# Position terms as row and column sums, another order of first loads and of the last comparisons, in a two-layer attention kernel

## The chip, the cores and the metric

The kernel runs on one core of one Trainium2 chip. A core has five engines with a queue of instructions each: TensorE (PE, matrix products; its weight loads are shown as PEld), VectorE (DVE), ScalarE (ACT), GpSimd (POOL) and SyncE (SP, which only issues transfers). Sixteen DMA engines move data between the device memory and the core's own memory, SBUF; matrix products land in another one, PSUM. The metric is the device time of one execution in microseconds (us).

## The reference

The input x is (8, 128, 48, 48): 8 batches, 128 channels, N = 48 x 48 = 2304 places. Cut to what matters:

```python
# layer 0: group norm, 32 position channels, q, k, v, causal attention
x0 = concat([gn(x), pe]).reshape(B, 160, N)
q = lrelu(Wq @ x0 + bq); k = lrelu(Wk @ x0 + bk); v = lrelu(Wv @ x0 + bv)
attn = softmax(where(tril, q.T @ k / sqrt(128), -10000)) * tril
x = x + attn @ v
# layer 1: on tokens
t = t + softmax(ln(t) @ ln(t).T) @ ln(t)
wx = batch_norm(ln(t) @ W.T)                 # over all 8 * 2304 tokens
y[s] = sigmoid(wx[s] + y[s - 1] @ V.T)       # a recurrence over the 2304 places
x = t + y
```

The position channels pe are 16 channels that depend on the row of a place alone and 16 that depend on its column alone; they are the same in all batches.

## The kernel before

All work is in float32. A batch's 2304 places are cut into NQ = 6 chunks of QC = 384 (eight rows of the image each). One program of three stages runs: an opening, the attention stream over the eight batches, and the recurrence. A general path (for inputs beyond certain bounds) stands behind a flag that the end of the fast path computes.

*Opening.* The first batch's x is loaded in three pieces on SP's queue (L706, L708), weights and position rows on ACT's and SP's queues (L733 to L739). Twelve products of a unit matrix with itself, written by `idle`, run on PE meanwhile. `positions(n, j)` (L820) makes the position term plus bias of chunk n for q, k and v (j = 0, 1, 2): the product of the 33 position weights (wpT) with the 33 position rows (L830; for v, places and channels are exchanged, in three products, L833), then a copy by ACT (L834). The three parts of a chunk are stored to the device memory together (posb_d, L836), and `load_positions` (L838) loads them back for every use but the first two. Chunks 0 and 1 are made in tiles of their own; the later ones share the two buffers of the pool tpool, one of which holds wpT. `group_norm` (L782) computes mean and reciprocal root for the norm: statistics on DVE, two tiny products on PE, a power on POOL (L660).

*The stream.* `project(b, n)` (L848) makes q, k and v of one chunk: norm on DVE (L865), product (L872, L875), addition of the position term (L877), leaky relu (L882). At its end DVE takes the largest absolute value of q and k (L886, for the flag). Three chunks are projected ahead (EARLY = 3). The class Causal runs layer 0's attention over pairs of a chunk and a block of 128 keys: score product (L1011), exp on ACT (L1013), a mask on POOL where the block lies on the diagonal (L1016), output product (L1022) three items later (LAG = 3), row sums on DVE (L1033, L1037). The class Full runs layer 1's attention, the residual, the norm and the product with W.

The order is written out by the class Stream, which has a clock of its own: `now`, and the time at which each engine is free. Side work is a chain of steps, each with an estimated cost and a due time; after every item `tick` runs at most two steps, the first in the list that are due. `finish` runs a chain to its end at once and moves `now` to its due time; `advance` runs it up to a step. The order so made is the order of the instructions on every engine; at run time each engine takes them in that order and waits where it must. Score products, projections and idle products take their PSUM tiles in turn from four buffers (psum_s).

*The recurrence.* 96 segments of LS = 24 places run side by side in three groups (G = 3), each begun 12 places early. DVE writes the inputs of two places into PSUM (L1488 to L1495), PE adds the product with V (L1539), ACT takes the sigmoid (L1541). Before it, PE runs fourteen idle products (L1471). The result of two places plus the residual is written by `add_residual` (L1517): on POOL up to place LM = 20 of a segment, on DVE behind it (groups 1 and 2 read a residual tile t2s with a stride, group 0 a tile t2l); group 0's earlier places are added by a DMA that POOL issues (L1553). `seams` (L1509) compares each segment's last state with the state that its right neighbour reached in its early places; the flag follows from the largest difference (L1558 to L1565), and each engine branches on it (L1578, L1579).

Of the kernel before, what the change touches and what calls it, by code (L numbers as in the profile page):

```python
# [14 lines left out]
F32 = mybir.dt.float32  # L15
# [6 lines left out]
EMB = 16  # L22
# [10 lines left out]
def position_rows(side):  # L33

    pe = np.array(
        [
            [p / np.power(10000.0, 2 * (j // 2) / EMB) for j in range(EMB)] if p != 0 else np.zeros(EMB)
            for p in range(side)
        ]
    )  # L40
    pe[1:, 0::2] = np.sin(pe[1:, 0::2])
    pe[1:, 1::2] = np.cos(pe[1:, 1::2])
    t = pe.astype(np.float32).reshape(EMB, side)
    px = np.broadcast_to(t[:, :, None], (EMB, side, side))
    py = np.broadcast_to(t[:, None, :], (EMB, side, side))
    ones = np.ones((1, side, side), np.float32)
    return np.ascontiguousarray(np.concatenate([px, py, ones], axis=0).reshape(NPE + 1, side * side))

# [499 lines left out]
class Stream:  # L548
# [48 lines left out]

    def finish(self, chain):
        while chain.steps:
            self.run(chain)  # L600
        self.now = max(self.now, chain.at)
# [3 lines left out]
def fast_path(ctx: ExitStack, tc: tile.TileContext, x, pe, w_ffn, out, x_tok, w_qkv, w_pos, v_t, gamma_beta, flag):  # L605
# [56 lines left out]
    with ExitStack() as actx:  # L662
# [78 lines left out]
        def ffn_weights():  # L741
# [4 lines left out]
            nc.vector.tensor_scalar(w1, w1, s, None, ALU.subtract)  # L746
            tp = psum_t("tp_ffn")
            nc.tensor.transpose(tp[:, 0:P], w1, ident)
            nc.vector.tensor_copy(w1T, tp[:, 0:P])
# [68 lines left out]
        pos, pos_loads, made = {}, {}, {}  # L818

        def positions(n, j):  # L820

            if j == 0:
# [4 lines left out]
            pe_c = pe_sb[n // (NQ // 2)][: NPE + 1, ts(n % (NQ // 2), QC)]  # L827
            ps = psum_s(f"pb_{n}_{j}")
# [5 lines left out]
            nc.scalar.copy(made[n][:, j, :], ps[:, :QC])  # L834
            if j == 2:
                nc.sync.dma_start(posb_d[:, n], made[n])  # L836
# [11 lines left out]
        def project(b, n):  # L848
# [18 lines left out]
            def part(j):  # L867
                def f():
# [15 lines left out]
                    if j == 2:  # L884
                        for i in range(2):
                            nc.vector.tensor_reduce(  # L886
                                largest[b][:, i, n : n + 1], c[i], AX.X, ALU.max, apply_absolute_value=True
                            )
# [7 lines left out]

            steps = [(normed, 0.0, [("DVE", 0.75)])]

            steps += [(part(j), QC * US, [("DVE", 0.0 if j < 2 else 4.5)]) for j in range(3)]
# [82 lines left out]
        class Causal:  # L982
# [133 lines left out]
        class Full:  # L1116
# [115 lines left out]
            def after(self, j, o):  # L1232
# [4 lines left out]
                far = FULL_FAR and not last  # L1237
# [150 lines left out]
        st.add([(ffn_weights, 0.3, [("DVE", 0.5)])], 30.0)  # L1388
# [53 lines left out]
    with ExitStack() as rctx:  # L1442
# [3 lines left out]
        rlast = rctx.enter_context(tc.tile_pool(name="rlast", bufs=3))  # L1446
# [24 lines left out]
        idle(pw[:, 2 * P :], 14)  # L1471
# [44 lines left out]

        def add_residual(g, l0, yt):  # L1517
# [12 lines left out]
        for t in range(-WARM, LS):  # L1530
            s = t % TZ
            for g in range(G):
# [89 lines left out]
```

## Time and profile before

| | us |
|---|---|
| median of 6 runs | 1783.17 |
| lowest and highest run | 1779.44 and 1785.31 |
| the profiled execution's own time | 1784.57 |
| its span, first to last instruction | 1782.7 |
| PE busy in the span | 1746.1 |
| DVE busy | 1312.9 |
| ACT busy | 734.2 |
| POOL busy | 204.6 |
| mean granted clock of PE | 0.99 |
| first score product starts | 19.36 |
| last statistics of the stream done | 1707.4 |
| first product of the recurrence starts | 1713.30 |
| last sigmoid ends | 1760.68 |
| last DVE add ends | 1775.32 |

The profile is of one execution. A line of its timeline has the start, the time taken, the engine, the line of the kernel, the operation, what it writes and reads, how often, and in brackets how long the engine had been idle before and what ended that. A line of a stage has its bounds and length, then busy time and number of instructions for PE, PEld, DVE, ACT and POOL, then the granted clock of PE (1.00 is full speed), the busy share of the DMA engines and GB/s. A float32 product shows as two instructions.

### The profile page before, as it was taken

To read this page: it belongs to the slowest core of one execution; us is meant where nothing else is said; L and a number is where in the kernel's file an instruction comes from. 1 tells how busy PE (TensorE), PEld (TensorE's weight loads), DVE (VectorE), ACT (ScalarE), POOL (GpSimd) and SP (SyncE) were. 2 spreads that over 40 slices of the span, in tenths; PEclk is the share of its full clock that TensorE was granted. 3 is DMA by queue.
4 is the path that set the end of the run, shared out by engine and by line. 5 is a ranking of instruction groups with operands and counts; after the bars stand their busy time and mean duration, and the time that the engine had idled before them with its cause. 6 is when DMAs were issued, how large, how long until landed. Compare 5 with 4: busy or idle time off the path is not lost.

```text
span 1782.7 us, 22180 instructions
## 1 busy us (share of the span) xinstructions
PE 1746.1 (98%) x6243; PEld 1095.3 (61%) x6243; DVE 1312.9 (74%) x3361; ACT 734.2 (41%) x1812; POOL 204.6 (11%) x305
## 2 busy tenths in 40 slices
PE   8999999999999999999999999999999999999995
PEld 5666566665666566665666656665666656665574
DVE  4868668766887668786688668786687866876477
ACT  2344424443345423444244433454234442454354
POOL 1110011100110001100111001100011001100026
PEclk8999999999999999999999999999999999999998
DMA  3405672257423584056622574245830576125847
GB/s 138 139 23 177 183 198 93 84 183 192 128 93 133 164 222 125 23 190 182 194 86 88 183 188 127 93 133 164 221 124 23 191 186 178 47 89 182 206 174 199
DMA packets 205576, 256.10 MB, mean 144 GB/s; under 512 B 89889, under 2 KB 175042, under 8 KB 205444
## 3 DMA queue, kind: packets, MB, share of 16 engines
q1 hardware_dynamic: 204492, 251.57, 48.0%
q0 software_dynamic: 720, 2.62, 1.0%
q8 instruction: 52, 0.85, 0.2%
q14 instruction: 80, 0.66, 0.1%
q10 hardware_dynamic: 232, 0.40, 0.1%
HBM read 150.24 MB, written 104.27 MB: 143 GB/s over the span
## 4 chain that ended last, share of the span: by engine, by line
PE 96%; DVE 1%; DMA 1%; issue 0%; ACT 0%; POOL 0%; SPq 0%; ACTq 0%; DVEq 0%; POOLq 0%
PE s L1212 18%; PE o L1226 18%; PE s L1011 17%; PE o L1022 17%; PE o L1222 13%; PE pj L872 4%; PE pj L875 2%; PE wx L1319 2%; PE z L1539 2%; PE tb L932 1%; PE of_t L932 1%; PE pb L830 0%; DVE r L1521 0%; DMA x<-in_x_dram 0%; PE dn L1070 0%
## 5 line engine op out<-in xcount | busy, mean ns | idle before, releaser
L1214 ACT ACTIVATE p<-s,shift 128x384 f32<-128x384 f32 x504 | 292.3, 580 | 487.5 <-PE s L1212 472.2
L1013 ACT ACTIVATE p<-s 128x384 f32<-128x384 f32 (+2 forms) x504 | 231.7, 460 | 440.9 <-PE s L1011 389.0
L1212 PE MATMUL s<-xh 128*128 128x384 f32 x1008 | 410.4, 489 | 0.0
L1226 PE MATMUL o<-p,xhT 128*128 128x384 f32 x1008 | 404.0, 487 | 4.4 <-ACT p L1214 4.4
L1011 PE MATMUL s<-q,k 128*128 128x384 f32 (+2 forms) x1008 | 382.1, 461 | 0.7 <-DVE k L882 0.7
L1022 PE MATMUL o<-p,vT 128*128 128x384 f32 (+2 forms) x1008 | 378.0, 457 | 0.0
L1222 PE MATMUL o<-g,xhT 128*128 128x384 f32 x720 | 281.4, 488 | 0.8 <-DMA g<-e 0.7
L1226 PEld LDWEIGHTS o<-p,xhT 128*128 128x128 f32 x1008 | 189.0, 190 | 132.3 <-ACT p L1214 8.7
L1022 PEld LDWEIGHTS o<-p,vT 128*128 128x128 f32 x1008 | 189.1, 191 | 115.1 <-issue 1.2
L1212 PEld LDWEIGHTS s<-xh 128*128 128x128 f32 x1008 | 186.1, 190 | 115.0
L1011 PEld LDWEIGHTS s<-q,k 128*128 128x128 f32 x1008 | 182.9, 191 | 98.1 <-issue 1.7
L1037 DVE TENSOR_TENSOR acc<-acc,p 128x384 f32<-128x384 f32 (+2 forms) x408 | 209.0, 512 | 33.4 <-POOL p L1016 8.8
L1175 DVE STREAM_TRANSPOSE t<-p 128x384 f32<-128x384 f32 x360 | 187.3, 550 | 37.6 <-ACT p L1214 36.0
L1222 PEld LDWEIGHTS o<-g,xhT 128*128 128x128 f32 x720 | 133.1, 190 | 83.3 <-issue 1.8
L1183 DVE TENSOR_REDUCE tsum<-t 128x12 f32<-128x1152 f32 x120 | 162.4, 1353 | 4.2
L877 DVE TENSOR_TENSOR z<-pj,pb 128x384 f32<-128x384 f32 x144 | 78.9, 548 | 111.2 <-PE pj L872 92.9
L1016 POOL TENSOR_TENSOR p<-p,triu 128x128 f32<-128x128 f32 x144 | 72.3, 504 | 609.1 <-ACT p L1013 496.7
L1292 POOL TENSOR_TENSOR roots<-ve_f,mhalf 128x3 f32<-128x3 f32 x48 | 41.1, 856 | 521.4 <-DVE ve_f L916 521.4
L1214 ACT ACTIVATION_READ_ACCUMULATOR p<-s,shift 128x1 f32 x504 | 97.2, 193 | 0.0
L872 PE MATMUL pj<-xn,wT 128*128 128x384 f32 x192 | 80.4, 504 | 1.4 <-DVE xn L865 1.4
L922 POOL TENSOR_TENSOR rs_c<-ve_c,mhalf 128x3 f32<-128x3 f32 x48 | 45.1, 940 | 216.2 <-DVE ve_c L916 213.6
L1320 DVE TENSOR_TENSOR scale<-wx,scale 128x384 f32<-128x384 f32 x46 | 25.4, 552 | 56.5 <-PE wx L1319 55.8
(264 smaller groups left out, 1475.3 us busy)
## 6 DMA issues: line engine op xcount, KB each, us to landing
e<-t SPq DMA_DIRECT2D x120, 576.0 KB
g<-e SPq DMA_DIRECT2D x480, 144.0 KB
pb<-posb_d SPq DMA_DIRECT2D x46, 576.0 KB
t1t<-in_x_tok_dram SPq DMA_DIRECT2D x48, 192.0 KB
t_d<-tt SPq DMA_DIRECT2D x184, 48.0 KB
t2x<-t_d SPq DMA_DIRECT2D x46, 192.0 KB
scale<-rs SPq DMA_DIRECT2D x46, 192.0 KB
x<-in_x_dram SPq DMA_DIRECT2D x14, 576.0 KB
```

Of the source, the lines that this page charges most:

```text
L872: nc.tensor.matmul(ps[:, :QC], wT[:, j, :], xn, start=True, stop=True)
L877: nc.vector.tensor_add(z, ps[:, :QC], c["pb"][:, j, :])
L1011: nc.tensor.matmul(s[:, off:QC], keys[b][:, ts(m, P)], queries[b, j][:, off:], start=True, stop=True)
L1013: nc.scalar.activation(p[:, off:], s[:, off:QC], AF.Exp, scale=SCALE)
L1022: nc.tensor.matmul(o[:, off:QC], vals[b][:, ts(m, P)], p[:, off:], start=first, stop=last)
L1037: nc.vector.tensor_add(a[:, off:], a[:, off:], p[:, off:])
L1175: nc.vector.transpose(t[:, :, :, g, :].rearrange("p b j r -> p j b r"), p.rearrange("p (j b r) -> p j b r", j=QB, b=R))
L1183: nc.vector.tensor_reduce(self.tsum[j][:, n - j - 1, :], t.rearrange("p b j m r -> p (b j) (m r)"), AX.X, ALU.add)
L1212: nc.tensor.matmul(s[:, :QC], xh[:, ts(m, P)], xh[:, ts(j, QC)], start=True, stop=True)
L1214: nc.scalar.activation(p, s[:, :QC], AF.Exp, bias=shift, accum_out=self.rows[:, m, j : j + 1])
L1222: nc.tensor.matmul(out_ap, xhT[:, QB * i + g, :], p, start=first, stop=last)
L1226: nc.tensor.matmul(o[:, :QC], xhT[:, what[1], :], p, start=first, stop=last)
```

## The change

- The position terms of q and k are no longer one product per chunk. A new input pe_rc (33 x 2 x 48) holds the row channels and the bias's one in its first part and the column channels in its second; `position_sums` makes the 2 x 48 terms of q and of k from it with two products and one copy, and `positions` adds a row's term and a column's term on POOL with operands that are repeated along one direction. v's part is made as before. In the opening the four parts for q and k of chunks 0 and 1 are made first, their v parts after the q and k products of chunk 0; for later chunks the order is v, q, k.
- On ACT's queue only the position weights and pe_rc are loaded ahead; the projection weights and both halves of the position rows come behind x on SP's queue.
- Idle products are written into the opening (9, 4 and 5) and ahead of chunks 1 and 2 of the first batch (8 each); ahead of the recurrence they are 8 instead of 14.
- The preparation of W (`ffn_weights`) becomes two steps, due at 40 instead of 30 on the stream's clock.
- The largest values of q and k become a step of their own; a chunk's items wait for the four steps ahead of it by a new `reach`, which moves `now` only when the chain stands just there.
- `far` in Full names one chunk more of the last batch (FULL_FAR is False).
- The DVE additions of the last four places of each segment come after the seams and the largest difference, all six in a row, with four buffers instead of three.

```diff
+def position_parts(side):
+    rows = position_rows(side)
+    parts = np.zeros((NPE + 1, 2, side), np.float32)
+    parts[:EMB, 0], parts[NPE, 0] = rows[:EMB, ::side], 1.0
+    parts[EMB:NPE, 1] = rows[EMB:NPE, :side]
+    return parts
...
+    def reach(self, chain, done):
+        self.advance(chain, done)
+        if chain.done == done:
+            self.now = max(self.now, chain.at)
...
+        SIDE = pe_rc.shape[-1]
+        rcs = gpool.tile([P, N // 2], F32, tag="g", name="rcs")
+        rc_sb = rcs[:, : 2 * SIDE]
         nc.scalar.dma_start(wpT[: NPE + 1], w_pos)
-        nc.scalar.dma_start(pe_sb[0][: NPE + 1, :], pe[:, : N // 2])
-        nc.scalar.dma_start(wT, w_qkv)
-        nc.sync.dma_start(pe_sb[1][: NPE + 1, :], pe[:, N // 2 :])
+        nc.scalar.dma_start(rc_sb[: NPE + 1, :], pe_rc.rearrange("k i s -> k (i s)"))
+        nc.sync.dma_start(wT, w_qkv)
+        for h in range(2):
+            nc.sync.dma_start(pe_sb[h][: NPE + 1, :], pe[:, ts(h, N // 2)])
...
+        rc = rcs[:, 2 * SIDE : 6 * SIDE].rearrange("p (j s) -> p j s", j=2)
+        def position_sums():
+            ps = psum_s("pb_rc")
+            for j in range(2):
+                nc.tensor.matmul(
+                    ps[:, ts(j, 2 * SIDE)], wpT[: NPE + 1, j, :], rc_sb[: NPE + 1, :], start=True, stop=True
+                )
+            nc.scalar.copy(rcs[:, 2 * SIDE : 6 * SIDE], ps[:, : 4 * SIDE])
...
             if j < 2:
-                nc.tensor.matmul(ps[:, :QC], wpT[: NPE + 1, j, :], pe_c, start=True, stop=True)
+                k = QC // SIDE
+                nc.gpsimd.tensor_add(
+                    made[n][:, j, :].rearrange("p (i s) -> p i s", s=SIDE),
+                    rc[:, j, ts(n, k)].unsqueeze(2).to_broadcast([P, k, SIDE]),
+                    rc[:, j, SIDE:].unsqueeze(1).to_broadcast([P, k, SIDE]),
+                )
             else:
+                pe_c = pe_sb[n // (NQ // 2)][: NPE + 1, ts(n % (NQ // 2), QC)]
+                ps = psum_s(f"pb_{n}_{j}")
                 for m in range(0, QC, P):
                     nc.tensor.matmul(ps[:, ds(m, P)], pe_c[:, ds(m, P)], wpT[: NPE + 1, j, :], start=True, stop=True)
-            nc.scalar.copy(made[n][:, j, :], ps[:, :QC])
-            if j == 2:
+                nc.scalar.copy(made[n][:, j, :], ps[:, :QC])
+            parts[n] += 1
+            if parts[n] == 3:
                 nc.sync.dma_start(posb_d[:, n], made[n])
...
-            steps += [(part(j), QC * US, [("DVE", 0.0 if j < 2 else 4.5)]) for j in range(3)]
+            steps += [(part(j), QC * US, [("DVE", 0.0 if j < 2 else 3.4)]) for j in range(3)]
+            steps.append((extremes, 0.0, [("DVE", 1.1)]))
...
-                    st.finish(projected[b, j])
+                    st.reach(projected[b, j], 4)
+                    if b == 0 and 0 < j < EARLY:
+                        idle(psum_s(f"idle_{j}"), 8)
                     if j + EARLY < NQ:
                         project(b, j + EARLY)
                     if j == NQ - 1:
+                        st.finish(projected[b, j])
                         bounds(b)
...
-                far = FULL_FAR and not last
+                far = FULL_FAR and not (b == B - 1 and j >= NQ - 3)
...
-        st.add([(ffn_weights, 0.3, [("DVE", 0.5)])], 30.0)
+        st.add([(ffn_centred, 0.0, [("DVE", 0.5)]), (ffn_turned, 0.12, [("DVE", 0.2)])], 40.0)
...
         idle(psum_s("idle"), 12)
-        for j in range(3):
-            positions(0, j)
+        position_sums()
+        for n in range(2):
+            for j in range(2):
+                positions(n, j)
+        idle(psum_s("idle_x"), 9)
         gn = st.add(group_norm(0))
         st.advance(gn, 2)
-        positions(1, 0)
+        idle(psum_s("idle_m"), 4)
         st.finish(gn)
-        for j in range(1, 3):
-            positions(1, j)
+        idle(psum_s("idle_v"), 5)
         project(0, 0)
-        making = st.add([(partial(positions, n, j), QC * US, [("ACT", 0.5)]) for n in range(2, NQ) for j in range(3)], 6.0)
+        st.advance(projected[0, 0], 3)
+        for n in range(2):
+            positions(n, 2)
+        making = st.add([
+            (partial(positions, n, j), 0.0 if j < 2 else QC * US, [("POOL", 1.0) if j < 2 else ("ACT", 0.5)])
+            for n in range(2, NQ) for j in (2, 0, 1)
+        ], 6.0)
...
-        rlast = rctx.enter_context(tc.tile_pool(name="rlast", bufs=3))
+        rlast = rctx.enter_context(tc.tile_pool(name="rlast", bufs=4))
...
-        idle(pw[:, 2 * P :], 14)
+        idle(pw[:, 2 * P :], 8)
...
+                    ys[g, l0] = y[g][:, so + 1 - TZ : so + 1]
                     if 0 <= l0 and (g or l0 >= LM):
-                        if t < LS - 1:
-                            add_residual(g, l0, y[g][:, so + 1 - TZ : so + 1])
+                        if l0 < LM:
+                            add_residual(g, l0, ys[g, l0])
...
-        for g in range(G):
-            add_residual(g, LS - TZ, y[g][:, TO[g] - TZ :])
-            if g:
+        for k, (l0, g) in enumerate((l, g) for l in range(LM, LS, TZ) for g in range(G)):
+            add_residual(g, l0, ys[g, l0])
+            if k:
                 continue
```

More of the change, by code (lines that the diff above doesn't have):

```diff
@@ L604, in fast_path @@
 @with_exitstack
-def fast_path(ctx: ExitStack, tc: tile.TileContext, x, pe, w_ffn, out, x_tok, w_qkv, w_pos, v_t, gamma_beta, flag):
+def fast_path(ctx: ExitStack, tc: tile.TileContext, x, pe, w_ffn, out, x_tok, w_qkv, w_pos, pe_rc, v_t, gamma_beta, flag):
     nc = tc.nc
@@ L739, in fast_path, with ffn_centred @@
         nc.sync.dma_start(gb, gamma_beta)
-        def ffn_weights():
+        def ffn_centred():
             s = small.tile([P, 1], F32, tag="gn_d", name="w_sum")
@@ L746, in ffn_weights, with ffn_turned @@
             nc.vector.tensor_scalar(w1, w1, s, None, ALU.subtract)
+        def ffn_turned():
             tp = psum_t("tp_ffn")
@@ L816, in fast_path @@
         keys, vals, queries, largest, projected = {}, {}, {}, {}, {}
-        pos, pos_loads, made = {}, {}, {}
+        pos, pos_loads, made, parts = {}, {}, {}, [0] * NQ
+        rc = rcs[:, 2 * SIDE : 6 * SIDE].rearrange("p (j s) -> p j s", j=2)
+        assert QC % SIDE == 0
+        def position_sums():
[5 more added lines that the diff above has]
+            nc.scalar.copy(rcs[:, 2 * SIDE : 6 * SIDE], ps[:, : 4 * SIDE])
         def positions(n, j):
-            if j == 0:
+            if n not in made:
                 if n < 2:
@@ L826, in positions @@
                     made[n] = tpool.tile([P, 3 * QC], F32, tag="t", name=f"pb_0_{n}").rearrange("p (j c) -> p j c", j=3)
-            pe_c = pe_sb[n // (NQ // 2)][: NPE + 1, ts(n % (NQ // 2), QC)]
-            ps = psum_s(f"pb_{n}_{j}")
             if j < 2:
-                nc.tensor.matmul(ps[:, :QC], wpT[: NPE + 1, j, :], pe_c, start=True, stop=True)
-            else:
+                k = QC // SIDE
[4 more added lines that the diff above has]
+                )
+            else:
+                pe_c = pe_sb[n // (NQ // 2)][: NPE + 1, ts(n % (NQ // 2), QC)]
+                ps = psum_s(f"pb_{n}_{j}")
                 for m in range(0, QC, P):
                     nc.tensor.matmul(ps[:, ds(m, P)], pe_c[:, ds(m, P)], wpT[: NPE + 1, j, :], start=True, stop=True)
-            nc.scalar.copy(made[n][:, j, :], ps[:, :QC])
-            if j == 2:
+                nc.scalar.copy(made[n][:, j, :], ps[:, :QC])
+            parts[n] += 1
+            if parts[n] == 3:
                 nc.sync.dma_start(posb_d[:, n], made[n])
@@ L884, in f @@
                     if j == 2:
[L885 to L888, printed above, removed]
                         load_positions(*divmod(b * NQ + n + 2, NQ))
@@ L895, in part, with extremes @@
                 return f
+            def extremes():
+                for i in range(2):
+                    nc.vector.tensor_reduce(largest[b][:, i, n : n + 1], c[i], AX.X, ALU.max, apply_absolute_value=True)
             steps = [(normed, 0.0, [("DVE", 0.75)])]
-            steps += [(part(j), QC * US, [("DVE", 0.0 if j < 2 else 4.5)]) for j in range(3)]
+            steps += [(part(j), QC * US, [("DVE", 0.0 if j < 2 else 3.4)]) for j in range(3)]
+            steps.append((extremes, 0.0, [("DVE", 1.1)]))
             c["chain"] = projected[b, n] = st.add(steps)
@@ L1515, in seams @@
             nc.vector.tensor_reduce(dm[:, g : g + 1], d[:, g, :, :n], AX.XY, ALU.max, apply_absolute_value=True)
+        ys = {}
         def add_residual(g, l0, yt):
@@ L1607 @@
         "w_pos": np.stack([np.vstack([i[:, C:].T, inputs[f"L0_conv_b{n}"][None]]) for i, n in zip(w, "qkv")], axis=1),
+        "pe_rc": position_parts(H),
         "v_t": inputs["L1_ffn_V"].T,
```

## The prediction

> **What bounds the kernel now.** I read the page, then the granted clock by stage, then the chain of waits and the timeline at both ends, because TensorE (PE) is busy for 98% of the span.
>
> ```profile
> span 1782.7 us, 22180 instructions
> PE 1746.1 (98%) x6243; PEld 1095.3 (61%) x6243; DVE 1312.9 (74%) x3361; ACT 734.2 (41%) x1812; POOL 204.6 (11%) x305
> ...
> 10.00:12.00 2.00, 1.69 (x5) 0.82 (x6) 0.70 (x4) 0.16 (x2) 0.00 (x0) 0.76 0.58 237
> ...
> 28.00:30.00 2.00, 0.95 (x3) 0.65 (x4) 1.22 (x5) 0.00 (x0) 0.60 (x1) 0.52 0.99 406
> ...
> 38.00:40.00 2.00, 2.00 (x10) 0.97 (x9) 0.18 (x1) 0.81 (x2) 0.00 (x0) 0.92 0.00 0
> ```
>
> The last three lines are stages; the figure third from the end is the granted clock. It is 0.5 from 11.0 to 17.9 us and from 28.2 to 38.3. In between and from there to 1765 it is 1.00. PE idles 36.6 us: some 22 after its last recurrent product (1760.3), 1.6 at the start, 1.5 at 27.55, 1.4 at 48.4, 3.2 around 1690 to 1706, and about 5 in all of 60 to 1690. So only the first 55 us and the last 75 have anything to give.
>
> ```profile
> 12.63 0.57 POOL L660 TENSOR_TENSOR gn_rs<-ve_gn,mhalf 128x1 f32<-128x1 f32 x1 [6.21 <-DVE ve_gn L659]
> ...
> 19.36 0.88 PE L1011 MATMUL s<-q,k 128*128 128x384 f32 x2 [0.67 <-DVE k L882]
> ...
> 31.20 0.32 SPq L843 DMA_DIRECT2D pb<-posb_d  x1
> ...
> 35.11 0.56 DVE L877 TENSOR_TENSOR z<-pj,pb 128x384 f32<-128x384 f32 x1 [5.26 <-DMA pb<-posb_d]
> ...
> 45.38 0.48 ACT L834 COPY pb<-pb 128x384 f32<-128x384 f32 x1 [2.02 <-DMA posb_d<-pb]
> ```
>
> These are timeline lines: start, duration, engine, what, and in brackets the idle time before and who ended it. The fourth shows a DVE wait that PE, at half clock, did not feel: chunk 3's positions had to be made, stored and loaded back. The fifth shows why they come late: making one chunk waits for the store of the chunk before it (one free buffer in tpool).
>
> ```profile
> 1757.27 6.44 DVE L1521 TENSOR_TENSOR r<-y,t2l 128x512 f32<-128x512 f32 x1 [0.35 <-ACT y L1541]
> ...
> 1761.64 6.09 POOL L1521 TENSOR_TENSOR r<-y,t2s 128x512 f32<-128x512 f32 x2
> ...
> 1763.63 5.42 DVE L1521 TENSOR_TENSOR r<-y,t2s 128x512 f32<-128x512 f32 x2
> ...
> 1771.83 0.68 DVE L1521 TENSOR_TENSOR r<-y,t2l 128x512 f32<-128x512 f32 x1
> ...
> 1772.56 2.76 DVE L1521 TENSOR_TENSOR r<-y,t2s 128x512 f32<-128x512 f32 x2
> ```
>
> At the end DVE adds take 6.44 and 2.7 us beside POOL's adds, and 0.68 (t2l) and 1.41 (t2s, minimum of that line) alone. The seams come only after them, at 1768.96.
>
> **Part 1, up to the first score product.** The x pieces land at 5.06, 7.10 and 8.79. By 8.8 us the windows add up to about 1.8 MB, of which x is 1.18. The three pieces with only 62 KB beside them, instead of 390 KB on the ACT queue, save 0.33 MB at some 0.29 MB/us: 1.1 us. This goes nowhere, since something else is late next. After the twelve idle products PE reaches position_sums at 7.02; four products of 96 columns and a copy of 192 columns (0.48 us for 384) end near 8.4. Then POOL does four adds of 128x384, and the power of L660 is queued behind them. No such add is in the trace. POOL's 128x128 product takes 0.448 us at least, its 128x512 add 1.517 at least; linearly, 384 columns take 1.16 (an estimate). The bounds are 0.45 and, by the 2.7 us of an add that shares its time with DVE, 2.0; I take 1.16, as the size lies between the two undisturbed rows. Adds end at 13.05, power 13.65, xn (0.48) 14.2: 0.5 later than the 13.72 of before.
>
> PE then does q0, k0, 12 products L833 (moved ahead of v0) and v0: three pairs of 0.65 and two groups of 0.86, 3.7 us at full clock, so the first score product is at 17.9. The idle products (9, 4 and 5, 0.11 us per half) end near 12.3, and PE has nothing for 2 us. If that costs the clock until 17.9, the product is at 19.7. I take the middle, 18.8, against 19.36; bounds 17.4 and 21.3.
>
> The Trainium skill (TensorE: Matmul & The Clock Gate, Part 1) says that the clock is halved after a free-running window of about 3.4 us with little work and restored after a busy one. The two slow stretches here, 6.8 and 10.2 us, are two and three of these. By that rule the place of the gap in a window decides between 17.9 and 19.7.
>
> **Part 2, the position round trip.** I followed the due times of the order by hand: chunk 2's parts are made after the first score item, chunk 3's after the second, and chunk 3 is projected ahead of chunk 2, as before. From the score product: exp and mask 1.94 (19.36 to 21.30), two adds 2.32, store 2.93 (22.93 to 25.86), two adds for chunk 3 2.32 (they wait for that store, and the masks behind them on POOL wait too; so does one copy on ACT with the exps behind it, which PE can spare), store until load 3.53 (27.67 to 31.20), load 3.91. z of chunk 3 is at 18.8 + 16.95 = 35.75, against 35.11. The 12 product pairs that are gone (8 of them in the stream, 0.84 each at full clock, 6.7 us) are not gained: PE runs dry near 33, as the next product, chunk 2's q, needs xn, which stands on DVE behind that z. It starts 1.7 later, at 37.4. From there PE has 11 pairs of 0.65, four short ones (1.3), two L833 groups (1.7), eight idle products (1.7), q and k of chunk 4 (1.3) and the turned w (0.15): 13.3, to 50.8. The dry stretch costs the clock for, I take, 5.1 us of the 3.4 to 6.8 that the two slow stretches suggest: 2.55. End 53.3. Before, the same work (through the product at 53.16) ended at 53.8. **Opening: -0.5**; bounds -4.5 (adds 1.0, clock kept) and +4.2 (21.3, adds 1.55).
>
> w1's part, split and due 10 us later, gives back the 1.5 us at 27.55, which PE now loses to xn of chunk 3. The maxima (1.08 per chunk on DVE) only move behind. In later batches PE is full, and both cost nothing; without that cover a chunk would pay 1.08. The edit of far does nothing, FULL_FAR being False (L773). On SP's queue nine loads are issued at the start instead of seven (0.33 to 0.45 us each), on ACT's two instead of three; wT and both halves of the position rows now come behind x and are first used after 14 us, so they are covered by the 2 MB that pass in the first 9 us and the idle DMA after it. The stores of chunks 0 and 1 move from 10 to some 19 us, ahead of chunk 2's at 23; if they were not done by then, each would hold it up by 0.58 MB at 0.4 MB/us, 1.4 us.
>
> **Part 3, before the recurrence.** Six idle products fewer are 12 halves of 0.115: 1.35. Inputs of the third group end at 1713.0 and can just be met, but those of the next step end near 15.9 and are needed at 15.66. **-1.05**; bounds 0 and -1.35.
>
> **Part 4, the end.** The recurrence ends at 1760.7; the seams can start at 1759.85. Alone, seams 2.6, off 0.35, six adds (2 x 0.68, 4 x 1.41) and flag follow to 1770.2, against 1775.32: -5.1. But POOL still has an add to finish and two to do. If the first subtraction is starved as the add at 1757.27 was (half its size: 3.1 us) and the other two run at the shared rate (1.3 each), the adds end at 1774.5: -0.8. I take **-2.5**, nearer the second, as POOL frees itself for a DMA at 1761. After the last add the 7 us to the end stay.
>
> The Trainium skill (GPSIMD Engine Reference, 4.1 Engine selection) speaks against moving the positions: it gives elementwise adds to VectorE, GpSimd being about two times slower. From its 4.50 us for 2048 elements one add would be an estimated 0.84 plus a start, and the sum would hardly change.
>
> **Sum:** -0.5 - 1.05 - 2.5 = -4.05 on the profiled 1784.57 (span 1782.7 and 1.9 around it): 1780.5. That execution lies 1.4 above the median of 1783.17, so I forecast 1783.17 - 4.05 = **1779.1**.
>
> **Rivals.** (1) *POOL becomes the bound* (slower): eight adds lie on the path, four ahead of the power, two and two in the round trip. Against: in the opening DVE mostly runs one-input statistics. For: the rows at 1763. At 2.0 each they cost 8 x 0.84 = 6.7 more, and the longer gap a clock stretch of 1.8: -4.05 + 8.5 = +4.5, 1787.7. It decides from 1.67 us an add. (2) *PE stays fed*: if the round trip is hidden, the stream gains 8 pairs (6.7), half clock (4.6) and idle (2.9), less 3.4 of new idle products, with 0.6 of the start: -11.4; with the ends 1768.2. For: PE is the chain's engine there. Against: the 5.26 us wait. (3) *Nothing arrives*: opening 0, the seams starved (-0.8), -0.6 from the shorter idle: 1781.8.
>
> **How the numbers follow.** Forecast 0.42 (own range 1775 to 1782), POOL 0.16, PE fed 0.14, nothing 0.28. A measurement of this kernel tells about 0.2% (3.6 us) from no change, so faster means below 1779.6. Of the forecast 0.30 lies there, of the fed case 0.14, of nothing 0.02: 0.46. Slower than 1786.7: 0.12 from POOL. Same: 0.42. The range of 1770 to 1786.5 leaves about 0.1 of each rival outside.
>
> **What would show it.** The power of L660 should start near 13 us, behind four POOL adds of 1.16. z of chunk 3 should wait for a load near 35 to 36, PE should be idle from 33 to 37 and at clock 0.5 after it; if PE is full there, rival 2 holds. The loop should begin a microsecond earlier relative to the last statistics. The first subtraction of the seams should last 1 to 3 us, the last add end 1 to 5 us sooner after the recurrence. Wrong would be: adds above 1.67, or a POOL power that does not wait.

## The result, and the profile after

The changed kernel takes 1785.5 us (median of 17 runs, 1780.0 to 1789.8), against 1782.7 of the kernel before on the same chip (39 runs, 1779.0 to 1787.5): ratio 1.0016, 95% interval 1.0008 to 1.0024. It is slower by 0.16%, where 1779.1 was forecast. The profiled execution grew by 2.4 us. Its page begins:

```profile
span 1785.1 us, 22216 instructions
...
PE 1739.0 (97%) x6279; PEld 1094.0 (61%) x6279; DVE 1314.1 (74%) x3361; ACT 728.3 (41%) x1801; POOL 218.7 (12%) x317
...
L1266 PE MATMUL o<-g,xhT 128*128 128x384 f32 x720 | 281.5, 489 | 9.5 <-DMA g<-e 9.5
```

PE has 7 us less work and still ends later. The third line, a group of instructions, has the reason after its last bar: before the turned products of layer 1 (L1222 before, L1266 now) PE idles 9.5 us for the blocks g that come back from device memory. (Layer 1's exponentials are symmetric; a block that was made once is turned by DVE, stored as e and loaded again as g, to serve as its mirror image.) Before, the idle time there was 0.8 us:

```profile
L1222 PE MATMUL o<-g,xhT 128*128 128x384 f32 x720 | 281.4, 488 | 0.8 <-DMA g<-e 0.7
```

Four stretches change, each read between two marks, after minus before:

| stage, mark | change in the profiled executions, us | the prediction |
|---|---|---|
| opening, first product of layer 1 in batch 0 (122.2 before) | -4.95 | -0.5 |
| the rest of the stream, to the last product of layer 1 | +10.2 | 0 |
| last statistics to last sigmoid (53.26 before) | -0.93 | -1.05 |
| last sigmoid to the end of the last instruction (21.93 before) | -1.84 | -2.5 |

They add up to +2.4. The 10.2 us come in steps: the difference at the first layer-1 product of batches 0 to 7 is -4.95, -2.86, -0.82, +0.58, +2.27, +2.48, +4.94, +4.93. The five large steps, in batches 0 to 3 and 5, have one PE wait of 1.1 to 2.5 us each, late in layer 1; the other two waits, of 0.4 us each, are in batch 7. The waits view (who waited for what: total, times, longest) shows SP's queue in the changed kernel:

```profile
SPq L883 <- DVE z L917: 49.1, 16, 7.1
...
SPq L1190 <- DMA pb<-posb_d: 16.1, 12, 2.3
```

The second line says that issues of g (L1190) stood 16.1 us behind a position load that was still moving. Before, the same wait was 0.6 us, once:

```profile
SPq L1146 <- DMA pb<-posb_d: 0.6, 1, 0.6
```

The first of the two lines above is SP's wait for a free buffer of the position terms, 15.0 us before. It is not what stalls PE: of the runs below, e11 has 43.3 us of it and no PE wait for g, and e10 has 3.2 us of it and 7.3 us of waits for g. The timeline of SP's queue around a seam, here the change from batch 0 to batch 1 (not the `seams` of the recurrence), shows how the transfers came to stand (start, duration, line, transfer, how many); first the kernel before:

```profile
234.34 3.69 SPq L1146 DMA_DIRECT2D g<-e  x8
238.13 0.38 SPq L843 DMA_DIRECT2D pb<-posb_d  x1
238.60 1.80 SPq L1146 DMA_DIRECT2D g<-e  x4
240.45 0.43 SPq L1310 DMA_DIRECT2D t2x<-t_d  x1
241.01 0.59 SPq L1312 DMA_DIRECT2D scale<-rs  x1
```

and the changed kernel:

```profile
229.12 1.80 SPq L1190 DMA_DIRECT2D g<-e  x4
231.02 0.38 SPq L883 DMA_DIRECT2D pb<-posb_d  x1
231.50 1.80 SPq L1190 DMA_DIRECT2D g<-e  x4
233.34 0.43 SPq L1354 DMA_DIRECT2D t2x<-t_d  x1
233.87 0.43 SPq L1356 DMA_DIRECT2D scale<-rs  x1
235.04 3.77 SPq L1190 DMA_DIRECT2D g<-e  x4
```

Four issues are one block g. Before, the blocks of rows 2 and 3 go out together, then the next batch's position load pb_3 (576 KB), then the block of row 4, then the token-major loads t2x and scale. After, pb_3 is ahead of the block of row 3, and t2x and scale are ahead of the block of row 4. All seven seams have this order, though not every one stalls: those behind batches 4 and 6 pass here without a wait, while in e16, the same kernel profiled again, the longest wait (2.9 us) is in batch 4. The chain of waits of the changed kernel at that place (start, duration, what):

```profile
232.87 7.10 DMA g<-e
239.97 0.14 issue
240.10 0.88 PE o L1266 x2
```

This is the block of row 3. Its last quarter was issued at 232.87, straight after the others, and lands 7.1 us later, behind the position load; PE, idle since 238.24, starts at 240.10. The issues that stand behind the position load at this seam are those of the block of row 4, not of this one.

### The profile page after: what moved, and what is told of

The parts are those of the page before. It is cut to its first block, busy times and chain, and to the rows that moved or that the text cites. A ratio compares the mean times of both kernels' runs of the same rounds, so it can differ in the third digit from the quotient of the medians.

```text
span 1785.1 us, 22216 instructions
## 1 busy us (share of the span) xinstructions
PE 1739.0 (97%) x6279; PEld 1094.0 (61%) x6279; DVE 1314.1 (74%) x3361; ACT 728.3 (41%) x1801; POOL 218.7 (12%) x317
## 4 chain that ended last, share of the span: by engine, by line
PE 94%; DMA 3%; DVE 2%; issue 1%; SPq 1%; ACT 0%; POOL 0%; DVEq 0%; ACTq 0%; POOLq 0%
PE s L1256 18%; PE o L1270 18%; PE o L1066 16%; PE s L1055 16%; PE o L1266 11%; PE pj L912 3%; DMA g<-e 2%; PE z L1593 2%; PE pj L915 2%; PE wx L1363 2%; PE tb L973 1%; PE of_t L973 1%; PE idle L1436 1%; SPq L1190 0%; PE dn L1114 0%
## 5 line engine op out<-in xcount | busy, mean ns | idle before, releaser
L1266 PE MATMUL o<-g,xhT 128*128 128x384 f32 x720 | 281.5, 489 | 9.5 <-DMA g<-e 9.5
L1266 PEld LDWEIGHTS o<-g,xhT 128*128 128x128 f32 x720 | 132.7, 190 | 93.8 <-issue 12.1
L1323 DVE SCALAR_TENSOR_TENSOR t<-of_t,ri,t1t 128x128 f32<-128x128 f32 x144 | 41.5, 344 | 38.3 <-PE of_t L973 38.3
```

Source lines behind the costliest of these rows:

```text
L1266: nc.tensor.matmul(out_ap, xhT[:, QB * i + g, :], p, start=first, stop=last)
```

## The experiments

Theory Q: the separate step for the maxima, and the 3.4 us that its predecessor counts in the model in place of 4.5, reorder SP's queue at the seams. Times are medians with the ratio to the kernel before on the same chip and its 95% interval. The rows come from several chips, on which the kernel before takes 1781.5 to 1783.2 us, so a difference of medians between two rows can be up to 1.7 us off; the ratios are free of this.

| run | us | ratio, interval | PE waits for g, us | half clock in the first 60 us | change at the opening's mark |
|---|---|---|---|---|---|
| before | 1781.5 to 1783.2 | | 0.7 | 17.1 | |
| changed | 1785.5 | 1.0016, 1.0008 to 1.0024 | 9.5 | 3.4 | -4.95 |
| e1, maxima merged again | 1778.96 | 0.9985, 0.9976 to 0.9993 | none | 6.8 | -1.98 |
| e2, before + split | 1791.38 | 1.0056, 1.0041 to 1.0072 | 5.6 | 10.2 | -4.48 |
| e3, position load later | 1783.94 | 1.0013, 1.0003 to 1.0023 | none | 17.1 | +3.86 |
| e4, split in batch 0 only | 1775.53 | 0.9965, 0.9952 to 0.9978 | none | 3.4 | -5.32 |
| e5, before + that split | 1782.01 | 0.9999, 0.9991 to 1.0008 | 1.7 | 17.1 | -1.94 |
| e6, before + the end | 1779.94 | 0.9985, 0.9976 to 0.9994 | 0.7 | 17.1 | +0.73 |
| e7, e4 without idle products | 1781.64 | 0.9996, 0.9988 to 1.0005 | 1.4 | 23.9 | -1.37 |
| e8, e4 with adds twice | 1782.30 | 1.0000, 0.9991 to 1.0009 | none | 13.7 | +1.53 |
| e9, e4 with 3.4 in the model | 1794.03 | 1.0064, 1.0051 to 1.0077 | 7.4 | 3.4 | -5.10 |
| e10, e4, load before g_3_5 | 1790.72 | 1.0042, 1.0027 to 1.0058 | 7.3 | 3.4 | -2.25 |
| e11, changed, 4.5 in the model | 1783.36 | 1.0001, 0.9993 to 1.0010 | none | 6.8 | -2.61 |
| e12, e6 + idle products | 1783.70 | 1.0004, 0.9995 to 1.0012 | 0.2 | 6.8 | +2.30 |
| e13, e4 with the old end | 1778.65 | 0.9979, 0.9970 to 0.9988 | 0.6 | 3.4 | -2.64 |
| e14, e4 with 16 idle products | 1779.86 | 0.9989, 0.9980 to 0.9998 | none | 3.4 | -2.55 |
| e15, e4 again | 1776.48 | 0.9969, 0.9958 to 0.9980 | none | 3.4 | -4.57 |
| e16, changed again | 1786.01 | 1.0019, 1.0009 to 1.0028 | 7.1 | 3.4 | -4.70 |

The last three columns are those of one profiled execution each; between kernels that are alike up to it (e4, e9, e10, e13, e15) the mark moves by 3 us, so what the opening is worth is read from the medians.

**e1, the maxima merged again.**

```diff
 if j == 2:
+    for i in range(2):
+        nc.vector.tensor_reduce(largest[b][:, i, n : n + 1], c[i], AX.X, ALU.max, apply_absolute_value=True)
     load_positions(*divmod(b * NQ + n + 2, NQ))
...
-steps += [(part(j), QC * US, [("DVE", 0.0 if j < 2 else 3.4)]) for j in range(3)]
-steps.append((extremes, 0.0, [("DVE", 1.1)]))
+steps += [(part(j), QC * US, [("DVE", 0.0 if j < 2 else 4.5)]) for j in range(3)]
...
-st.reach(projected[b, j], 4)
+st.finish(projected[b, j])
```

> The changed kernel with the maxima back behind v, in the step that had them before (4.5 us in the model, and the chain finished where its chunk begins). Theory Q (the split of the chain's last step reorders SP's queue near each batch's seam, so that the loads of turned blocks g_3_5 and g_4_5 stand behind a position load of 576 KB and two loads of the token-major part): the waits of 1.1 to 2.5 us before the turned products (9.5 us in 7 waits) go, the stream loses nothing against the kernel before, and the time is 1782.7 - 4.95 (opening) - 2.8 (end) = about 1775. Rival T (the stalls come from the earlier opening, which shifts batches against each other, or from contention): the 9.5 us stay, about 1785. Rival M (the separate maxima made the opening's gain): the stalls go, but the opening's 4.95 shrinks to under 2.5, about 1778.

1778.96. The waits for g are gone, and layer 1 of batches 0 to 6 takes what it took before, within 0.3 us each. But the time is 4 us above the 1775 that Q gives, and the opening shows 1.98 in place of 4.95: both Q and M hold (by the medians the split is worth 3.4 us against e4, on the same chip, and 2.5 against e15).

**e2, the split alone in the kernel before** (the reverse of e1's diff, put on the kernel before).

> The kernel before with the maxima's split alone, and nothing else of the change. Theory Q: SP's order at each seam is that of the changed kernel, so the waits before the turned products come up (about 9 us in 7 of the 8 batches), and the time is about 1783 + 10 = 1793 (1789 to 1795). Rival T: about 1783, the turned products' wait stays at 0.7 us. Rival M: under 1783, as the opening's products start earlier, 1780.

1791.38, 9 us slower, by nothing but this split. The trace has the changed kernel's order at the seams and 5.6 us of waits for g. Rival T falls. The profiled execution, of 1786.3, is the lowest of six: in it the stream loses 6.9 us, and where the median loses 5 us more was not seen.

**e3, the position load later.**

```diff
-        load_positions(*divmod(b * NQ + n + 2, NQ))
...
 def extremes():
     for i in range(2):
         nc.vector.tensor_reduce(...)
+    load_positions(*divmod(b * NQ + n + 2, NQ))
```

> The changed kernel with the issue of the next position load moved from part 2 of the chain into the separate maxima's step. g_3_5 stands ahead of the position load again, as in the kernel before, but g_4_5 is still behind the two loads t2x_3 and scale_3. Theory Q with the position load (576 KB) as the costly one: most of the stalls go, 1776 to 1779. With the two loads of the token-major part, or with the later issue of g itself, as the costly one: the stalls stay, 1783 to 1786. Rival T: 1785.

1783.94 fits the second answer, but the trace says the first: PE has no wait for g, and the difference to before stays within 4.2 and 3.8 us from batch 1 to batch 7. With the position load behind the block of row 3, and the block of row 4 still behind t2x and scale, nothing stalls. The time was lost elsewhere: in batch 0 the loads now come too late (z of chunk 3 waits 9.8 us for its load), and the opening loses 3.9 us in place of gaining 4.95.

**e4, the split in batch 0 only.**

```diff
 if j == 2:
+    if b:
+        extremes()
     load_positions(*divmod(b * NQ + n + 2, NQ))
...
-steps += [(part(j), QC * US, [("DVE", 0.0 if j < 2 else 3.4)]) for j in range(3)]
-steps.append((extremes, 0.0, [("DVE", 1.1)]))
+steps += [(part(j), QC * US, [("DVE", 0.0 if j < 2 else 4.5 if b else 3.4)]) for j in range(3)]
+if b == 0:
+    steps.append((extremes, 0.0, [("DVE", 1.1)]))
```

> The changed kernel with the maxima's split in batch 0 alone, and merged again in batches 1 to 7. Theory Q: SP's order at the seams is that of the kernel before, the opening keeps all its gain: about 1775, and at or below the run with the maxima merged everywhere. Rival T: 1785. Rival M: 1775, and 2.5 us or more below the run with the maxima merged everywhere.

1775.53, the best version of this study, and the number Q gave. Its line for the turned products, with no idle time:

```profile
L1269 PE MATMUL o<-g,xhT 128*128 128x384 f32 x720 | 281.1, 488 | 0.0
```

**e9 and e10, the order alone.** e9 changes one figure of e4's model, e10 one due time; neither adds, removes or splits an instruction. e9's figure moves instructions in every queue (PE's order differs from e4's in 147 places). e10 is the clean one: its queues are those of e4 on PE, DVE, ACT and POOL, instruction by instruction, and SP's differs by seven swaps.

```diff
-[("DVE", 0.0 if j < 2 else 4.5 if b else 3.4)]      # e9
+[("DVE", 0.0 if j < 2 else 3.4)]
...
-pos_loads[b, n] = st.add([(f, 0.0, [])], st.free["DVE"] - st.now)      # e10
+pos_loads[b, n] = st.add([(f, 0.0, [])], st.free["DVE"] - (b > 0 and n == 3) * 1.1 - st.now)
```

> The run with the maxima split in batch 0 alone, and one number of the order's model changed in it: the last step of a projection counts 3.4 us of DVE work in batches 1 to 7 too, as in the changed kernel, while the maxima stay in that step. No instruction is added, removed or split; only the order of issue changes. Theory Q (the order does it): SP's queue at each seam is that of the changed kernel, its waits before the turned products come back, about 1785 (1782 to 1787). Rival (the separate step itself, its tick and its place on DVE, does it): 1775.5.

> The run with the maxima split in batch 0 alone, and one swap in SP's queue at each of the seven seams: the position load pb_3 of the next batch is issued ahead of the turned block g_3_5 and not behind it; g_4_5 stays ahead of t2x_3 and scale_3. Theory Q with the position load as the costly one: waits before the turned products, 0.7 to 1.4 us a seam, 5 to 10 us in all, 1780.5 to 1785. Rival (g_4_5 behind the two token-major loads, or the later issue of both, is the costly one): 1775.5, at most 1 us more.

e9 takes 1794.03, 18.5 us more than e4. In its profile the stream loses 10.2 us (from -5.10 to +5.11), as in the changed kernel. e10 takes 1790.72, by one swap a seam; SP's timeline in e4:

```profile
228.09 3.70 SPq L1193 DMA_DIRECT2D g<-e  x8
231.89 0.38 SPq L883 DMA_DIRECT2D pb<-posb_d  x1
233.01 1.73 SPq L1193 DMA_DIRECT2D g<-e  x4
234.79 0.43 SPq L1357 DMA_DIRECT2D t2x<-t_d  x1
```

and in e10:

```profile
231.06 3.02 SPq L1193 DMA_DIRECT2D g<-e  x4
234.18 0.38 SPq L883 DMA_DIRECT2D pb<-posb_d  x1
234.65 6.57 SPq L1193 DMA_DIRECT2D g<-e  x8
241.55 0.34 SPq L1357 DMA_DIRECT2D t2x<-t_d  x1
```

Eight issues of g took 3.70 us without the position load ahead of them and 6.57 behind it; most of the difference is one issue, the last, which waited 2.8 us for that load. The chain of e10 has the last quarter of the block of row 3, which SP issued without a wait, and PE's timeline the consequence in its brackets (idle time before, and what ended it):

```profile
236.02 7.47 DMA g<-e
```

```profile
243.62 1.62 PE L1269 MATMUL o<-g,xhT 128*128 128x384 f32 x2 [2.64 <-DMA g<-e]
```

and e10's waits of SP's queue have the sum over the run:

```profile
SPq L1193 <- DMA pb<-posb_d: 16.1, 10, 2.8
```

So the costly swap is the position load ahead of a block that PE needs in the next few us; the token-major loads are not (e3). In e10 the clock adds to it: right behind the first of these waits PE is at half clock from 243.22 to 246.63. Both runs cost more than was expected, e10 by 5.7 us over its range and e9 by 7. e9's profiled execution, of 1787.2, is the lowest of its six; where its median loses 6.8 us more was not seen. The size of the loss varies from execution to execution: e10's six lie between 1784.0 and 1792.8, e4's five between 1775.0 and 1776.3.

**e11, the changed kernel with the old figure in the model.**

```diff
-steps += [(part(j), QC * US, [("DVE", 0.0 if j < 2 else 3.4)]) for j in range(3)]
-steps.append((extremes, 0.0, [("DVE", 1.1)]))
+steps += [(part(j), QC * US, [("DVE", 0.0 if j < 2 else 4.5)]) for j in range(3)]
+steps.append((extremes, 0.0, [("DVE", 0.0)]))
```

> The changed kernel with the maxima still split off in all batches, but with the model's figures set so that the position loads come due as before: 4.5 us for the last step of the projection, 0 for the maxima's own step. SP's order at the seams is that of the kernel before. Theory Q: about 1775.5 (within 1.5 us of the run split in batch 0 alone). Rival (the separate step does it): 1785.

The stalls are gone, as Q has it, with the separate step kept, so the step itself is not what stalls. SP's order is that of the kernel before at four of the seven seams only; at the other three it is e3's, with the block of row 4 behind t2x and scale. At none is the position load ahead of the block of row 3. The time is missed by 8 us: the opening gains only 2.61, and behind the first layer-1 product of batch 7 another 2.9 us go (-0.96 there, +1.98 at the last one). There PE waits, and then has half clock from 1695.37 to 1698.78, as e4 has not; what opens that gap is not settled.

**e5, the split of batch 0 in the kernel before** (e4's diff against e2).

> The kernel before with the maxima split off in batch 0 alone, nothing else of the change. Theory Q: SP's order at the seams stays, and the opening's gain of the run with the split everywhere (4.5 us at the first Full product) is kept to the end: 1782.1 - 4.5 = about 1777.6. Rival (the split's gain is the difference between the changed kernel with the maxima split in batch 0 and with them merged, 3.4 us): 1778.7. Rival (what the split gains in the opening is only moved and comes back as waits later): 1782.

1782.01, no change. The split gains 2.5 to 3.4 us where the rest of the opening is changed (e1 against e15 and e4), and nothing measurable alone.

**e6 and e13, the end alone and the end undone.**

```diff
-rlast = rctx.enter_context(tc.tile_pool(name="rlast", bufs=3))      # e6
+rlast = rctx.enter_context(tc.tile_pool(name="rlast", bufs=4))
-idle(pw[:, 2 * P :], 14)
+idle(pw[:, 2 * P :], 8)
...
-if t < LS - 1:      # e6; e13 takes this back in e4
+if l0 < LM:
...
-for g in range(G):
-    add_residual(g, LS - TZ, y[g][:, TO[g] - TZ :])
-    if g:
+for k, (l0, g) in enumerate((l, g) for l in range(LM, LS, TZ) for g in range(G)):
+    add_residual(g, l0, ys[g, l0])
+    if k:
```

> The kernel before with the end's part of the change alone: 8 idle products instead of 14 ahead of the recurrence, the seams compared before the residuals of the last steps, four buffers for these. Theory: what the changed kernel's trace shows after the last statistics (75.8 to 73.0 us) comes from these edits alone, -2.8, about 1779.3. The sum of the prediction's two terms would be -3.55, 1778.6. Rival (the end's gain is a side effect of the shifted stream): 1782.

> The run with the maxima split in batch 0 alone, with the end's old order: the residuals of the last places but two are added as they come, the seams compared after them (8 idle products and four buffers kept). Theory: of the 2.8 us of the end alone, 0.9 come from the idle products and 1.9 from the order of the seams, so this run is 1775.5 + 1.9 = 1777.4. The prediction's term for the order would make it 1778.0. Rival (the order is worth nothing, as the first subtraction is starved by POOL's adds): 1775.5.

e6: 1779.94, -2.8 as the traces had said. e13: 1778.65, 2.2 us over e15, or 3.1 over e4; by the ratios 1.8 and 2.5, with intervals that overlap. The traces are sharper: from last sigmoid to end e13 has 21.98 us, against 19.95 in e4, so the order of the recurrence's seams is worth 2.0, and the six idle products 0.9.

**e7, e12 and e14, the idle products.** e7 leaves those of the opening out of e4 (the 8 of chunks 1 and 2 too), e12 puts them into e6 (positions still on PE), e14 doubles those of chunks 1 and 2.

```diff
-idle(psum_s("idle_x"), 9)      # e7 takes these out, e12 adds them
...
-idle(psum_s("idle_m"), 4)
...
-idle(psum_s("idle_v"), 5)
...
 if b == 0 and 0 < j < EARLY:
-    idle(psum_s(f"idle_{j}"), 8)
+    idle(psum_s(f"idle_{j}"), 16)      # e14
```

> The changed kernel with the maxima split in batch 0 alone, without the idle products of the opening except the first 12 (left out: 9, 4, 5 and twice 8). Theory C (they keep the clock up: half clock 3.4 us in the changed kernel's opening against 17.1 us before): the clock falls in the gaps, about 14 us more at half clock in an opening where PE waits much of the time: 3 us lost, 1778.5. Rival: PE is behind DVE there in any case, and the products cost as much as they save: 1775.5, within 1 us.

> The kernel before with the end's part of the change and the opening's idle products (9, 4, 5 and twice 8) added between its own products, positions still made on PE, x still second. Theory C1 (the idle products alone make the opening's gain, by the clock): half clock in the opening from 10.2 to 3.4 us, 4 us gained on the run with the end alone: 1776. Theory C2 (the room for them comes from the position products taken off PE; put into a full PE they delay as much as they save): 1779 to 1782.

> The run with the maxima split in batch 0 alone, with 16 idle products in place of 8 at the begin of chunks 1 and 2 in batch 0. Theory C (the opening's time follows the half clock that its gaps bring): the one stretch of 3.4 us at half clock goes, up to 1.7 us gained, and PE's gaps of 2.6 and 2.0 us are filled: 1774 to 1775.5. Rival (products in front of the waiting ones delay what they should serve): 1776 to 1777.5.

The windows of 12 to 36 us (PE busy, ..., granted clock third from the end), in e4:

```profile
12.00:24.00 12.00, 9.54 (x50) 6.63 (x50) 8.82 (x17) 2.97 (x7) 4.23 (x6) 1.00 0.44 157
24.00:36.00 12.00, 9.06 (x37) 6.36 (x37) 5.00 (x12) 0.98 (x2) 1.50 (x3) 0.86 0.43 156
```

and in e7:

```profile
12.00:24.00 12.00, 11.65 (x33) 8.11 (x34) 4.95 (x10) 2.18 (x5) 2.16 (x3) 0.50 0.24 98
24.00:36.00 12.00, 9.06 (x26) 5.32 (x24) 5.34 (x10) 1.28 (x4) 3.66 (x5) 0.74 0.60 213
```

In the first of the two stages PE runs 50 instructions (idle products among them) in 9.54 us at clock 1.00 in e4, and 33 in 11.65 us at 0.50 in e7. Without the idle products the kernel is 6.1 us over e4 (5.2 over e15), back at the time before. e12 shows that they do nothing by themselves: half clock falls from 17.1 to 6.8 us, but among the position products they delay the work, and the time is 3.8 over e6. e14 fell to its rival: the slow stretch of 3.4 us stays, and the time is 3.4 over e15. Not all of this is the opening's. In the profiled executions e14 is 2.0 us behind e15 at the opening's mark and loses another 2.6 in layer 1 of batch 7, where its clock is at half from 1692.54 to 1695.95 and e15's is not; e12 has such a stretch as well, from 1697.43 to 1700.84, and e6 has none. Whether the idle products bring it about was not tested.

**e8, the POOL adds of chunks 0 and 1 twice.**

```diff
-nc.gpsimd.tensor_add(...)
+for _ in range(2 if n < 2 else 1):
+    nc.gpsimd.tensor_add(...)
```

> The changed kernel with the maxima split in batch 0 alone, and each of the four POOL adds of chunks 0 and 1 done twice. Theory P (POOL's adds stand ahead of its power and so of the normalised x): 4 x 0.80 = 3.2 us more on POOL, of which 0.7 us were idle there: xn 2.5 us later, and 2.5 us at the end, 1778. Rival (the first product's delay is taken up by PE's later gaps of 2.6 and 2.0 us, where it waits for DVE): 1775.5 to 1776.5.

POOL's timeline in the changed kernel:

```profile
7.67 3.19 POOL L863 TENSOR_TENSOR pb<-rcs 128x384 f32<-128x384 f32 x4 [1.22 <-ACT rcs L852]
11.58 0.57 POOL L675 TENSOR_TENSOR gn_rs<-ve_gn,mhalf 128x1 f32<-128x1 f32 x1 [0.73 <-DVE ve_gn L674]
```

and in e8:

```profile
7.94 6.81 POOL L864 TENSOR_TENSOR pb<-rcs 128x384 f32<-128x384 f32 x8 [1.51 <-ACT rcs L852]
14.71 0.57 POOL L675 TENSOR_TENSOR gn_rs<-ve_gn,mhalf 128x1 f32<-128x1 f32 x1
```

With eight adds the power waits for POOL and for nothing else, and starts 3.1 us later than in the changed kernel. The whole kernel takes 6.8 us more than e4 (5.8 more than e15): PE idles 2.9 us before its first product of the projections, at 15.90, and half clock grows from 3.4 to 13.7 us. Theory P had the place right and half the size.

**e15 and e16, the repaired and the changed kernel side by side.** The kernels of e4 and of the change, as they are.

> The run with the maxima split in batch 0 alone, once more and on the chip at hand now, as the measure for the runs made after it (the old end, more idle products). If its 1775.5 holds: ratio 0.9965 within 0.001, 1775 to 1777. If it was one chip's or one hour's: 1778 to 1780, and then neither the old order of the seams nor the sixteen idle products cost anything that was measured.

> The changed kernel itself, on the same chip as the run with the maxima split in batch 0 alone. Theory Q: waits before the turned products of about 9 us in 6 or 7 seams, and 1785 to 1790, some 9 us or more above that run. Rival: within 3 us of it.

1776.48 and 1786.01 on one chip: what the split does in batches 1 to 7 costs 9.5 us of the median. e13 and e14 are read against e15, which ran on another chip than they did.

## Why the prediction was wrong

**The step that failed** is "The maxima (1.08 per chunk on DVE) only move behind. In later batches PE is full, and both cost nothing; without that cover a chunk would pay 1.08." The term for the stream was 0, and 10.2 us were measured. The prediction priced the DVE instructions that move. The split also changes a figure of the model from which the whole order is written, and the 1.1 us reach SP's queue in seven batches. e9 makes that visible, as it moves no maximum out of its step in batches 1 to 7 and costs 18.5 us; e10 shows that one swap a seam in SP's queue is enough (15.2 us over e4); e4 takes the effect away and gains 10 us on the changed kernel. The due times had been followed by hand for the opening and not for a seam. None of the rivals had this mechanism; rival 1 had a figure near the result for another reason, and its POOL is not the bound: four adds end before the power can start.

**The opening: right in sign, a tenth of the size.** Term "-0.5", measured -4.95. Three figures in it were off. The add took 0.80 us, not 1.16, so the power started at 11.58, behind DVE and not behind the adds, and the first score product at 16.53, not 18.8. The clock was not lost in the gap ahead of it. And z of chunk 3 came at 31.91 and not at 35.75, with 3.4 us at half clock in all in place of 5.1; it waits for its load there, as forecast (issued at 28.17, landed at 31.82). "PE runs dry" was right in kind: PE idles 2.60 and 1.71 us at 25.6 and 33.6, both times for a normalised x on DVE. "The maxima only move" was wrong here as well, on the good side: of the opening's gain 2.5 to 3.4 us are the split's (e1 against e15 and e4).

**Before the recurrence: right.** -1.05 predicted, -0.93 measured (53.26 to 52.33, in e6 alone too).

**The end: right in sum, wrong in place.** -2.5 predicted, -1.84 measured, 2.0 in e13. DVE's timeline after (the seams' subtractions L1564, the last adds L1575):

```profile
1764.14 3.60 DVE L1564 TENSOR_TENSOR d<-y,warm 128x248 f32<-128x248 f32 x1 [2.94 <-ACT y L1595]
...
1769.52 1.34 DVE L1564 TENSOR_TENSOR d<-y,warm 128x248 f32<-128x248 f32 x1
...
1771.31 0.40 DVE L1564 TENSOR_TENSOR d<-y,warm 128x248 f32<-128x248 f32 x1
...
1776.52 2.76 DVE L1575 TENSOR_TENSOR r<-y,t2s 128x512 f32<-128x512 f32 x2
```

The first subtraction is starved as in the less favourable of the two cases (3.1 predicted, 3.60), and the adds end only 0.3 us sooner after the last sigmoid (14.32, 14.63 before). The gain sits where "the 7 us to the end stay" was written: last add to end is 5.8 us in place of 7.3.

With the opening and the end as they turned out and no loss in the stream, the sum would have been 7.7 us below before, near 1775; that is where e4 lies.

## What to carry to other kernels

Where a program writes its own order from modelled costs, a changed cost is an edit of every queue: lay the issue order of each DMA queue beside the old one, at the places where a load is needed soonest, before pricing the instructions. A large load that nobody needs yet must not stand ahead of a small one that the bounding engine needs soon; here the small one took 7.1 and 7.5 us from issue to landing. Apply such an edit only where its gain is: here batch 0 alone kept the whole gain.

## What was not expected of the hardware

- A POOL add of 128x384 whose two inputs are both broadcast took 0.80 us (four in 3.19) and 0.85 (eight in 6.81), less than a line between the 0.448 of 128 and the 1.517 of 512 columns gives. The estimate of 0.84 us plus a start, from the 4.50 us for 2048 elements in the Trainium skill (GPSIMD Engine Reference, 3.1 Elementwise — side-by-side cycle accounting), which the prediction had set aside, was nearer. The advice of the same page (4.1 Engine selection) against elementwise adds on GpSimd did not decide here, as four adds end before the power's input is ready.
- A DMA issue of SP can wait for the transfer ahead in its queue: 16.1 us in 12 waits behind position loads in the changed kernel, 2.8 us in a single issue of e10. A load that is issued behind it without a wait can still keep PE waiting: it landed 7.1 us after its issue in the changed kernel, 7.5 in e10.
- Every slow clock stretch of the opening, in every run, lasted one to five times 3.41 us (from 3.4 in e4 to 17.1 in e7), which agrees with the window of about 3.4 us that the Trainium skill states (TensorE: Matmul & The Clock Gate, Part 1). A delay of 3.1 us on POOL became 5.8 to 6.8 us of the whole, with 10.2 us more at half clock. The place of a stretch goes with the time as well, in five profiles of one opening (e4, e9, e15, e10 and e13): it gains 5.3, 5.1 and 4.6 us where the one slow stretch begins at 25 to 27 us, and 2.3 and 2.6 where it begins at 34 to 35.
- In the last windows of 2 us with stores they moved at 137 to 152 GB/s with the old end (e13) and at 249 to 274 with the new one (e4), where the last add is followed by the end of the span 1.7 us sooner. Why is open.
